# A two-layer mixer and experts kernel: blocks of two sizes, a wide last stage, u·B in two places, gates apart, a table of offsets

## The chip, the cores and the metric

The kernel runs on one core of a Trainium2 chip. The metric is the device time of one execution in microseconds, lower is better. Engines have short names throughout: PE is the matrix engine (PEld its weight loads), DVE the vector engine, ACT the scalar engine, POOL the GpSimd engine, SP the engine that issues most DMAs.

## What is computed

Two layers over x of shape (4, 256, 64, 64), that is 16384 tokens of 256 channels, all in float32. Cut to what matters here:

```python
# layer 0: a Mamba mixer, with d = 512 inner channels and 16 states each
tokens = x_as_tokens @ w_in.T
z = sigmoid(silu(tokens @ w_gate.T + b_gate))
t = layernorm(tokens)
xm, zm = split(t @ in_w.T)
xm = silu(conv4(xm)); dt = softplus(...); B, C = ...
h = exp(dt * A) * h + (dt * xm) * B          # along 4096 tokens, per (channel, state)
y = sum_over_states(h * C) + D * xm
y = (y * silu(zm)) @ out_w.T
x = tokens + (y * z) @ w_out.T + x
# layer 1: a state-space mixer with 8 heads, then a mixture of 8 experts
t = tokens(x);  t = t + mixer1(layernorm(t))
idx = argmax(softmax(layernorm(t) @ gate_w + gate_b)); prb = its probability
pos = place of the token among those of its expert, kept if pos < C = 2560
y_tok = relu(buf @ w1[e] + b1[e]) @ w2[e] + b2[e]   # 256 -> 1024 -> 256
t = t + nan_to_num(y_tok * prb * kept);  out = t as (4, 256, 64, 64)
```

The recurrence of layer 0 is the large part: 4 × 4096 tokens × 512 channels × 16 states.

## The kernel before, in words

Three stages run one after another: the mixers of both layers, the experts, and a last stage that turns token rows into channel rows.

*Mixers.* The tokens go by in 64 chunks of 256 (four images of 16). For each chunk the recurrence is done in 16 units. A unit handles 128 partitions (4 states × 32 channels) and a free size of 4 × 256. In `scan` (from line 837) unit u = j × 4 + f does the following: four ACT exponentials write the decay tile `da`; DVE multiplies `u4` by B (a tensor_tensor) into `ub`, a tile of 4 KB per partition in two banks of PSUM of which there is one copy (`bank_u`, depth 1); if the chunk isn't an image's first, a short DVE tensor_tensor adds the carried state `e0` into the first column of `ub`; DVE runs tensor_tensor_scan over `da` and `ub` into `h` (SBUF, three copies); POOL multiplies `h` by C into `p` (two copies); PE sums `p` over states into `py`. Every second j, `gx`, a tile of gates and of the inputs that pass by the recurrence, is loaded by two DMAs of 256 KB (two copies of 8 KB per partition). ACT writes the passing half, scaled by D, into `py`, and DVE multiplies `py` by the gate half into `g`.

While a chunk's units run, other parts of this chunk and of earlier and later ones are done between them: `front0` and `mid0` (projections, convolution, dt), `tail0`, `front1`, `ssd` and `back1` (layer 1 and the routing). Each part carries a due time in units, set by `k_.at(n)`: the constants `FRONT0`, `MID0`, `TAIL`, `SSD`, `BACK` give the parts their place, and `SHIFT` could give single calls of `at` an offset, by their number within a chunk. It is empty before.

The order of instructions on every engine is planned while the program is built, by the class `Plan`: a list scheduler with a weight for each instruction (`dve`, `act`, `mm`, ...), a delay for a result to be seen by another engine (`SIGNAL`) or by its own (`BEHIND`), the depth of each ring of tiles, and one resource that DVE and POOL share, called the port. A DVE operation holds the port in the plan if more than one of its tensor inputs lies in SBUF; a scan never does. A POOL operation always does. The multiplication by C is marked `ride`: it is put at the start of a scan, and in the program it waits for the DVE instruction just ahead of that scan.

At the end of the mixers, DVE works out from the counts of the experts a table: for each of 71 blocks of 256 rows which rows of the routed buffer it holds (`row_at`) and which expert's weights (`w_at`).

*Experts.* For each block (`begin(i)` and the loop after it, from line 1335): POOL gathers rows and one expert's weights (4360 floats per partition, three buffers) by indirect DMA, ACT normalizes, PE transposes, then PE does the first layer in 8 pieces of 128 hidden channels (ACT and DVE apply bias and relu) and the second layer; DVE and ACT clean up the result, POOL scatters it into `tok_d`. The next block's `begin` is placed in the middle of the first layer.

*Last stage* (`turn`): 32 pieces of 512 tokens. SP loads rows from `tok_d` so that a partition holds every 128th token (runs of 1 KB), PE transposes them, DVE and ACT in turn copy the result out of PSUM, ACT's queue stores 2 KB runs.

Of the kernel before, what the change touches and what calls it, by code (L numbers as in the profile page):

```python
# [20 lines left out]
P = 128  # L21
# [21 lines left out]
MID0 = -16  # L43
TAIL, SSD, BACK = 18, 29, 37
AHEAD = 4

SHIFT = {}
TOK = 4
# [88 lines left out]
class Plan:  # L137
# [6 lines left out]
    SIGNAL = {"DVE": 0.13, "ACT": 0.19, "PE": 0.21, "POOL": 0.12}  # L144
    BEHIND = {"DVE": 0.13, "ACT": 0.14, "PE": 0.0, "POOL": 0.13}
    LANES = 8
# [237 lines left out]
def tile_conv_attn_hybrid(ctx: ExitStack, tc: tile.TileContext, a: dict, out: bass.AP, cap: int, st: int):  # L384
# [12 lines left out]
    def nm(s):  # L397
        return f"{s}_{next(names)}"
# [10 lines left out]
    make_identity(nc, ident)  # L409

    nj = st // P
    nblk = NT // st + NE - 1
    row_at = const.tile([P, nblk, nj], U32, name="row_at")
    w_at = const.tile([P, nblk], U32, name="w_at")

# [10 lines left out]
    def mixers(es):  # L426
# [138 lines left out]
        def work(shape, tag, bufs=1):  # L565
            return r.tile(lambda: wk.tile(shape, F32, name=nm(tag), tag=tag, bufs=bufs), shape, tag, bufs)
# [76 lines left out]

        routed, rows_at, ws_at = r.fixed(buf_d), r.fixed(row_at), r.fixed(w_at)

# [191 lines left out]
        def scan(k_):  # L837
# [10 lines left out]
            for j in range(KD):  # L848
# [11 lines left out]
                if j % 2 == 0:  # L860

                    gx = work([P, 2, 2, T], "gx", 2)
                    for s in range(2):
                        r.dma("SP", gx[:, s], k_.gx_d[s * KD + j : s * KD + j + 2].rearrange("j p l -> p j l"))
                sl = slice(j * SQ, (j + 1) * SQ)
# [7 lines left out]
                for f in range(SQ):  # L873
# [6 lines left out]
                    k_.at(u)  # L880
                    ub = bank_u(SQ, T)
                    r.tt(ub, u4, bc[:, 0, None, :].to_broadcast([P, SQ, T]), ALU.mult)
# [10 lines left out]
                    if f == 0:  # L893
                        if j % 2 == 0:
                            py = bank_y(2, T)
                            for i in range(2):
                                r.act(py[:, i], gx[:, 1, i], AF.Copy, scale=m_d[:, j + i : j + i + 1])
                    for i in range(SQ):
# [11 lines left out]
                if j % 2 == 1:  # L910
                    r.tt(k_.g[:, j - 1 : j + 1], gx[:, 0], py, ALU.mult)

# [374 lines left out]
        def iota(t, step, n, cm=0):  # L1287
            r.gps("iota", t, [[step, n]], 0, cm, allow_small_or_imprecise_dtypes=True)
            return t
# [4 lines left out]

        per = cap // st
        steps, block, which_e = iota(line(0, per), st, per), iota(line(0, nblk), 1, nblk), iota(line(0, NE), 1, NE)
        place = iota(line(0, nj), P, nj, 1)
        counts, one, blocks, ends, starts = (line(0, NE) for _ in range(5))
        which, count, base, limit = (line(0, nblk) for _ in range(4))
        some = line(0, NE, per)  # L1300
        r.gps("memset", one, 1.0)
        r.copy(counts, total)
        r.tt(some, over(counts, (NE, per), True), over(steps, (NE, per), False), ALU.is_gt)
        r.dve("tensor_reduce", blocks, some, AX.X, ALU.add)
        r.dve("tensor_tensor_scan", ends, one, blocks, 0.0, ALU.mult, ALU.add)
        r.tt(starts, ends, blocks, ALU.subtract)
        n = (nblk, NE)
        table = line(1, *n)
        r.tt(table, over(block, n, True), over(ends, n, False), ALU.is_ge)
        r.dve("tensor_reduce", which, table, AX.X, ALU.add)  # L1310
        mine = line(2, *n)
        r.tt(mine, over(which, n, True), over(which_e, n, False), ALU.is_equal)
        for sums, values in ((base, starts), (count, counts)):
            r.tt(table, mine, over(values, n, False), ALU.mult)
            r.dve("tensor_reduce", sums, table, AX.X, ALU.add)

        r.tt(base, block, base, ALU.subtract)
        r.dve("tensor_scalar", base, base, float(st), None, ALU.mult)
        r.dve("scalar_tensor_tensor", count, count, float(cap), base, ALU.min, ALU.subtract)
        r.dve("scalar_tensor_tensor", base, which, float(cap), base, ALU.mult, ALU.add)  # L1320
        r.dve("tensor_scalar", base, base, float(NSLOT), None, ALU.subtract)
        n = (nblk, nj)
        row, valid = line(2, *n), line(2, *n)
        r.tt(valid, over(count, n, True), over(place, n, False), ALU.is_gt)
        r.tt(row, over(base, n, True), over(place, n, False), ALU.add)
        r.tt(row, row, valid, ALU.mult)
        r.dve("tensor_scalar", rows_at, row, float(NSLOT), None, ALU.add)
        r.dve("tensor_scalar", which, which, float(NE - 1), float(P), ALU.min, ALU.mult)
        r.tt(ws_at, which, place[:, :1].to_broadcast([P, nblk]), ALU.add)
        r.issue()  # L1330

    def experts(es):
# [19 lines left out]

        def begin(i):

            w = wp.tile([P, W1 + W2 + KF + C], F32, name=nm("w"), tag="w")
            rows = wk.tile([P, nj, ROW], F32, name=nm("rows"), tag="rows", bufs=4)
            for j in range(nj):
                gather(rows[:, j], buf_d, row_at[:, i, j : j + 1], NSLOT + P)
            gather(w, a["w_exp"], w_at[:, i : i + 1], NE * P)
            tn = wk.tile([P, nj, C], F32, name=nm("tn"), tag="tn")  # L1360
            for j in range(nj):
                act(tn[:, j], rows[:, j, TOK:], AF.Identity, scale=rows[:, j, 1:2], bias=rows[:, j, 2:3])  # L1362
            number = wk.tile([P, nj], U32, name=nm("number"), tag="number", bufs=4)
            nc.vector.tensor_copy(number, rows[:, :, 3])  # L1364
            xt = wk.tile([P, KC, st], F32, name=nm("xt"), tag="xt")
            pt = pt_p.tile([P, KC, st], F32, name=nm("pt"), tag="pt")
            for k in range(KC):
                for j in range(nj):
                    nc.tensor.transpose(pt[:, k, j * P : (j + 1) * P], tn[:, j, k * P : (k + 1) * P], ident)
            nc.vector.tensor_copy(xt, pt)  # L1370
            return w, rows, number, xt

        now = begin(0)
        for i in range(nblk):
            w, rows, number, xt = now
# [3 lines left out]
            b2 = w[:, W1 + W2 + KF :]  # L1379
            hid = wk.tile([P, KF, st], F32, name=nm("hid"), tag="hid")  # L1380
            for f in range(KF):
                if f == KF // 2 and i + 1 < nblk:

                    now = begin(i + 1)
                ph = ph_p.tile([P, st], F32, name=nm("ph"), tag="ph")
                for k in range(KC):
                    mm(ph, w1[:, k, f * P : (f + 1) * P], xt[:, k], start=k == 0, stop=k == KC - 1)  # L1387
                if f % 4 != 3:
                    act(hid[:, f], ph, AF.Relu, bias=b1[:, f : f + 1])  # L1389
                else:  # L1390
                    ts(hid[:, f], ph, b1[:, f : f + 1], 0.0, ALU.add, ALU.max)
            y = wk.tile([P, nj, C], F32, name=nm("y"), tag="y")
            fixed = wk.tile([P, nj, C], F32, name=nm("fixed"), tag="fixed")
            ok = wk.tile([P, nj, C], U32, name=nm("ok"), tag="ok", bufs=1)
            po = po_p.tile([P, nj, C], F32, name=nm("po"), tag="po")
            for j in range(nj):
# [22 lines left out]
    def turn(es):  # L1419

        wk = es.enter_context(tc.tile_pool(name="out_work", bufs=6))
        pt_p = es.enter_context(tc.tile_pool(name="out_ps", bufs=6, space=PSUM))
        W = 512
        nj = W // P
        for b in range(NB):
            for c in range(L // W):
                i = b * L + c * W
                rows = wk.tile([P, nj, C], F32, name=nm("outrows"), tag="outrows")
                nc.sync.dma_start(rows, tok_d[i : i + W].rearrange("(j p) d -> p j d", p=P))  # L1429
                o = wk.tile([P, KC, W], F32, name=nm("o"), tag="o")  # L1430
                for k in range(KC):
                    pt = pt_p.tile([P, W], F32, name=nm("pto"), tag="pto")
                    for j in range(nj):
                        nc.tensor.transpose(pt[:, j * P : (j + 1) * P], rows[:, j, k * P : (k + 1) * P], ident)  # L1434
                    if k % 2 == 0:
                        nc.vector.tensor_copy(o[:, k], pt)  # L1436
                    else:
                        nc.scalar.copy(o[:, k], pt)  # L1438
                nc.scalar.dma_start(out[b].rearrange("(k p) l -> p k l", p=P)[:, :, c * W : (c + 1) * W], o)  # L1439
# [103 lines left out]
```

## Time and profile before

| what | us |
|---|---|
| median of 3 runs | 6741.11 (6736.48 to 6754.15) |
| the profiled execution's own time | 6746.82 |
| its span, first to last instruction | 6745.1 |
| mixers, to the last entry of the routing table | 5611 |
| experts, to the last block's scatter | 5611 to about 6652 |
| last stage | 6653.7 to 6745 |

The span and the shares of the page are of one execution. A group line gives the line of the kernel, the engine, the operation, what it writes and reads, the sizes, the count, the busy time in us with the mean of one in ns, and the idle time of the engine just ahead with what ended most of it. Nearly all the mixers' instructions have line 373, since the planner issues them all from there; so they are told apart by the tiles they write. A window line gives busy time and count for PE, PEld, DVE, ACT and POOL, then the granted clock of PE, the mean busy share of the 16 DMA engines and what they moved in GB/s. Where DVE or POOL is held up inside an instruction, no idle time is shown: the instruction only has a longer duration. The granted clock over the execution was 0.957.

### The profile page before, as it was taken

Reading aid. Unit: us, or ns where it says so; the run is one execution under the profiler, and the core shown is the slowest. Engines: PE = TensorE matmul, PEld = TensorE weight load, DVE = VectorE, ACT = ScalarE, POOL = GpSimd, SP = SyncE. Lnnn points to the kernel's source line nnn. Section 1 sums busy time; section 2 is a strip of 40 time slices with the busy share of each in tenths; the row PEclk is TensorE's granted clock in tenths of the full one; section 3 lists DMA queues with packets and bytes.
Section 4 is the critical chain, followed back from the end, with each engine's and each line's share of the span. In section 5 each row is a group of like instructions: output and inputs, shape, how many; then the busy total and the mean of one; then the engine's idle time right before and its main releaser. Section 6 shows DMA issues by size and latency. Waiting matters only on the chain. (4 is left out here: it accounts for less than half of the span.)

```text
span 6745.1 us, 111880 instructions
## 1 busy us (share of the span) xinstructions
PE 6239.9 (93%) x37672; PEld 4330.6 (64%) x37672; DVE 5559.2 (82%) x7646; ACT 4878.5 (72%) x12007; POOL 3305.5 (49%) x2632
## 2 busy tenths in 40 slices
PE   7899999999999999999999999999999978999996
PEld 5566666666666666666666666666666546888886
DVE  5999999999999999999999999999999973344443
ACT  6888888888878888888888888888888852333332
POOL 4655555555555555555555555555555542333331
PEclk8999999999999999999999999999999988999998
DMA  6855555555555555555555555555555534555556
GB/s 189 233 151 149 151 149 151 149 147 151 152 148 153 149 148 152 152 153 152 149 150 151 151 153 147 156 151 151 153 149 150 148 92 158 186 196 190 193 191 243
DMA packets 943874, 1077.19 MB, mean 160 GB/s; under 512 B 94480, under 2 KB 912404, under 8 KB 934082
## 3 DMA queue, kind: packets, MB, share of 16 engines
q1 hardware_dynamic: 904594, 842.28, 45.0%
q0 software_dynamic: 30000, 210.98, 8.7%
q10 hardware_dynamic: 8704, 16.78, 0.6%
q8 instruction: 297, 4.87, 0.3%
q14 instruction: 279, 2.29, 0.1%
HBM read 785.70 MB, written 277.68 MB: 158 GB/s over the span
## 5 line engine op out<-in xcount | busy, mean ns | idle before, releaser
L373 POOL TENSOR_TENSOR p<-h,bc 128x1024 f32<-128x1024 f32 x1024 | 2413.7, 2357 | 1996.7 <-DVE ub L373 501.3
L373 DVE TENSOR_TENSOR_SCAN h<-da,ub 128x1024 f32<-128x1024 f32 x1024 | 2339.1, 2284 | 77.0 <-ACT da L373 4.4
L373 ACT ACTIVATE da<-dt,w_m_Alog 128x255 f32<-128x255 f32 x4096 | 1842.7, 502 | 0.0
L373 DVE TENSOR_TENSOR ub<-u,bc 128x1024 f32<-128x1024 f32 x1024 | 1279.1, 1249 | 13.9 <-DMA u<-u_d 6.5
L373 PE MATMUL py<-p,sum 128*32 128x256 f32 x8192 | 658.9, 394 | 175.1 <-POOL p L373 168.8
L373 PE MATMUL b<-t,w_W_in 128*128 128x256 f32 x2304 | 579.0, 392 | 25.2 <-ACT bcs L373 4.8
L373 PEld LDWEIGHTS b<-t,w_W_in 128*128 128x128 f32 x2304 | 418.4, 190 | 188.7 <-ACT raw L373 75.3
L1387 PE MATMUL ph<-xt,w 128*128 128x256 f32 x2272 | 516.3, 381 | 4.0 <-ACT hid L1389 3.9
L373 PE MATMUL a<-t,w_m_in_w 128*128 128x256 f32 x2048 | 513.4, 395 | 3.0 <-DVE t L373 2.7
L1398 PE MATMUL po<-w,hid 128*128 128x256 f32 x2272 | 502.0, 379 | 0.0
L373 PEld LDWEIGHTS py<-p,sum 128*32 128x32 f32 x8192 | 169.0, 108 | 497.3 <-POOL p L373 246.5
L373 PE MATMUL a<-raw,taps_m 128*128 128x256 f32 x2048 | 482.0, 383 | 4.9 <-ACT pre L373 4.9
L1398 PEld LDWEIGHTS po<-w,hid 128*128 128x128 f32 x2272 | 431.7, 190 | 58.7
L1387 PEld LDWEIGHTS ph<-xt,w 128*128 128x128 f32 x2272 | 427.0, 191 | 62.2 <-ACT hid L1389 5.7
L373 PEld LDWEIGHTS a<-t,w_m_in_w 128*128 128x128 f32 x2048 | 372.8, 191 | 145.6 <-issue 72.5
L373 PEld LDWEIGHTS a<-raw,taps_m 128*128 128x128 f32 x2048 | 378.2, 190 | 130.4 <-ACT e L373 39.8
L373 ACT COPY hlast<-h 128x4 f32<-128x4 f32 x1024 | 202.9, 198 | 273.6 <-DVE h L373 260.9
L1364 DVE CAST number<-rows 128x2 uint32<-128x2 f32 x71 | 12.0, 169 | 467.0 <-DMA tok_d<-fixed,number 455.5
L1362 ACT ACTIVATE tn<-rows 128x256 f32<-128x256 f32 x142 | 82.3, 597 | 402.9 <-DMA rows<-buf_d,row_at 397.2
L373 PE MATMUL c<-cum,after 128*128 128x512 f32 x512 | 323.8, 719 | 15.9 <-ACT dend L373 13.5
L1410 POOL DMA_INDIRECT tok_d<-fixed,number x142 | 146.1, 1029 | 391.2 <-DVE fixed L1408 308.5
L373 ACT ACT_TABLE_LOAD x256 | 328.4, 1283 | 4.5
(237 smaller groups left out, 11320.5 us busy)
## 6 DMA issues: line engine op xcount, KB each, us to landing
dt<-dt_d SPq DMA_DIRECT2D x1024, 128.0 KB, 2.8
u<-u_d SPq DMA_DIRECT2D x1024, 128.0 KB, 2.2
raw<-raw_d SPq DMA_DIRECT2D x1024, 128.0 KB, 3.6
gx_d<-pre SPq DMA_DIRECT2D x64, 1024.0 KB, 5.5
bc<-bc_d SPq DMA_DIRECT2D x1024, 64.0 KB, 2.4
gx<-gx_d SPq DMA_DIRECT2D x256, 256.0 KB, 4.8
raw_d<-raw SPq DMA_DIRECT2D x64, 518.0 KB, 3.6
dt_d<-mid SPq DMA_DIRECT2D x64, 512.0 KB
```

Of the source, the lines that this page charges most:

```text
L373: op.issued = f(*map(placed, args), **{k: placed(v) for k, v in kw.items()})
L1362: act(tn[:, j], rows[:, j, TOK:], AF.Identity, scale=rows[:, j, 1:2], bias=rows[:, j, 2:3])
L1364: nc.vector.tensor_copy(number, rows[:, :, 3])
L1387: mm(ph, w1[:, k, f * P : (f + 1) * P], xt[:, k], start=k == 0, stop=k == KC - 1)
L1398: mm(po[:, j], hid[:, f, j * P : (j + 1) * P], w2[:, f], start=f == 0, stop=f == KF - 1)
L1410: nc.gpsimd.indirect_dma_start(out=tok_d, out_offset=bass.IndirectOffsetOnAxis(ap=number[:, j : j + 1], axis=0), in_=fixed[:, j], in_offse ...
```

## The change

Five things are changed at once.

1. `ub` of even units is a tile in SBUF (`ub1`, one copy), that of odd units stays in PSUM.
2. `gx` is split in two tiles of 4 KB, `pass` and `gate`, one copy each, with load times of their own. The SBUF that this frees is what `ub1` takes.
3. `SHIFT` gets 13 offsets, `SSD` and `BACK` come one unit earlier, and the plan's delay of a DVE result to DVE (`BEHIND`) goes from 0.13 to 0.17.
4. The experts' 71 blocks of 256 rows become 63 of 256 (two units of 128) and 9 of 128, with a routing table for each size; the small ones are spread among the large.
5. The last stage works on 16 pieces of 1024 tokens. A partition holds 8 consecutive tokens (a run of 8 KB), so the copies out of PSUM write with a stride of 8 elements, and stores go in 4 KB runs.

```diff
-TAIL, SSD, BACK = 18, 29, 37
+TAIL, SSD, BACK = 18, 28, 36
-SHIFT = {}
+SHIFT = {
+    18: -0.2, 41: 0.5, 47: 5.9, 50: -1.7, 51: -0.5, 58: -6.4, 63: 1.1, 97: -0.9, 108: 1.0, 111: 0.2, 120: -9.8,
+    130: -1.0, 137: -0.2,
+}
-    BEHIND = {"DVE": 0.13, "ACT": 0.14, "PE": 0.0, "POOL": 0.13}
+    BEHIND = {"DVE": 0.17, "ACT": 0.14, "PE": 0.0, "POOL": 0.13}
...
     nj = st // P
-    nblk = NT // st + NE - 1
-    row_at = const.tile([P, nblk, nj], U32, name="row_at")
-    w_at = const.tile([P, nblk], U32, name="w_at")
+    units = NT // P + NE - 1
+    n_big = (units - NE) // 2
+    sizes = (nj, n_big), (1, units - nj * n_big)
+    tables = [
+        (const.tile([P, n, k], U32, name=f"row_at{k}"), const.tile([P, n], U32, name=f"w_at{k}")) for k, n in sizes
+    ]
...
-                    gx = work([P, 2, 2, T], "gx", 2)
-                    for s in range(2):
-                        r.dma("SP", gx[:, s], k_.gx_d[s * KD + j : s * KD + j + 2].rearrange("j p l -> p j l"))
+                    both = []
+                    for s, name, n in ((1, "pass", -AHEAD), (0, "gate", 3)):
+                        k_.at(j * SQ + n)
+                        t = work([P, 2, T], name)
+                        r.dma("SP", t, k_.gx_d[s * KD + j : s * KD + j + 2].rearrange("j p l -> p j l"))
+                        both.append(t)
+                    passed, gate = both
...
-                    ub = bank_u(SQ, T)
+                    ub = bank_u(SQ, T) if u % 2 else work([P, SQ, T], "ub1")
...
-                                r.act(py[:, i], gx[:, 1, i], AF.Copy, scale=m_d[:, j + i : j + i + 1])
+                                r.act(py[:, i], passed[:, i], AF.Copy, scale=m_d[:, j + i : j + i + 1])
...
-                    r.tt(k_.g[:, j - 1 : j + 1], gx[:, 0], py, ALU.mult)
+                    r.tt(k_.g[:, j - 1 : j + 1], gate, py, ALU.mult)
...
+        upto_here(ends, starts, pairs)
+        r.dve("tensor_scalar", taken, starts, -1.0, float(n_big), ALU.mult, ALU.add)
+        r.dve("scalar_tensor_tensor", taken, taken, 0.0, pairs, ALU.max, ALU.min)
+        r.dve("scalar_tensor_tensor", rest, taken, -2.0, n_units, ALU.mult, ALU.add)
+        r.dve("tensor_scalar", gone, taken, float(st), None, ALU.mult)
+        for (k, nblk), (rows_at, ws_at), n_blocks, behind in zip(sizes, tables, (taken, rest), (zero_e, gone)):
+            rows_at, ws_at = r.fixed(rows_at), r.fixed(ws_at)
+            upto_here(ends, starts, n_blocks)
...
-        now = begin(0)
-        for i in range(nblk):
+        line_up = sorted(((i + 0.5) / n, k, i) for k, n in sizes for i in range(n))
+        now = begin(*line_up[0][1:])
+        for at, (_, nj, _) in enumerate(line_up):
+            st = nj * P
...
-        wk = es.enter_context(tc.tile_pool(name="out_work", bufs=6))
+        wk = es.enter_context(tc.tile_pool(name="out_work", bufs=4))
-        W = 512
+        W = 1024
         nj = W // P
+        half = nj // 2
...
-                nc.sync.dma_start(rows, tok_d[i : i + W].rearrange("(j p) d -> p j d", p=P))
+                nc.sync.dma_start(rows, tok_d[i : i + W].rearrange("(p j) d -> p j d", p=P))
...
+                    for h in range(2):
+                        pt = pt_p.tile([P, half, P], F32, name=nm("pto"), tag="pto")
+                        for j in range(half):
+                            nc.tensor.transpose(pt[:, j], rows[:, h * half + j, k * P : (k + 1) * P], ident)
+                        to = o[:, k].rearrange("c (p j) -> c j p", j=nj)[:, h * half : (h + 1) * half]
```

The rest of the routing table (which expert a block belongs to, its rows) is worked out as before, once for each of the two sizes.

## The prediction

> **What bounds the kernel now.** I read the page first, then the chain of waits, the windows, the groups by form, and last the timeline.
>
> ```profile
> span 6745.1 us, 111880 instructions
> PE 6239.9 (93%) x37672; PEld 4330.6 (64%) x37672; DVE 5559.2 (82%) x7646; ACT 4878.5 (72%) x12007; POOL 3305.5 (49%) x2632
> ```
>
> The shares mix three stages. The chain of waits doesn't help: its 73 pieces begin at 6624 us, inside the last stages. So I go by windows (busy time and count of PE, PEld, DVE, ACT, POOL; clock; DMA share; GB/s):
>
> ```profile
> 4760.00:4930.00 170.00, 159.46 (x1017) 103.98 (x1016) 160.96 (x216) 141.31 (x353) 93.07 (x71) 0.97 0.55 155
> ...
> 5655.00:6650.00 995.00, 984.25 (x4685) 864.22 (x4683) 408.82 (x762) 316.76 (x686) 347.12 (x338) 1.00 0.52 185
> ...
> 6695.00:6715.00 20.00, 12.66 (x72) 10.82 (x71) 5.57 (x9) 3.85 (x8) 0.00 (x0) 0.76 1.08 385
> ```
>
> The mixers (to 5611 us) keep DVE at 161 of 170 us and PE at 159, the experts (to 6650) keep PE at 99%, and the last stage keeps the DMA engines full at 385 GB/s. The mixers hold four fifths of the span. Their costliest groups:
>
> ```profile
> L373 POOL TENSOR_TENSOR p<-h,bc 128x1024 f32<-128x1024 f32 x1024 | 2413.7, 2357 | 1996.7 <-DVE ub L373 501.3
> L373 DVE TENSOR_TENSOR_SCAN h<-da,ub 128x1024 f32<-128x1024 f32 x1024 | 2339.1, 2284 | 77.0 <-ACT da L373 4.4
> ...
> L373 DVE TENSOR_TENSOR ub<-u,bc 128x1024 f32<-128x1024 f32 x1024 | 1279.1, 1249 | 13.9 <-DMA u<-u_d 6.5
> ```
>
> The tile view of h has the first scan at 82.4 us and the last at 5506.2: 5424 us for 1024 units, 5.30 us a unit, 84.8 us for a chunk of 16. POOL's p takes 2.36 us per unit, and whether it fits beside DVE decides everything below. The timeline shows when it does and when it doesn't (start, duration, engine):
>
> ```profile
> 394.50 2.36 POOL L373 TENSOR_TENSOR p<-h,bc 128x1024 f32<-128x1024 f32 x1 [0.69 <-DVE cdec L373]
> ...
> 395.54 2.40 DVE L373 TENSOR_TENSOR decay<-decay,gm 128x1024 f32<-128x1024 f32 x1
> 396.80 1.19 POOL L373 COPY raw<-tail_raw 128x12 f32<-128x12 f32 x1
> ...
> 397.86 0.67 DVE L373 TENSOR_TENSOR g<-gx,py 128x512 f32<-128x512 f32 x1
> 398.11 2.36 POOL L373 TENSOR_TENSOR p<-h,bc 128x1024 f32<-128x1024 f32 x1
> 398.46 3.10 DVE L373 TENSOR_TENSOR ub<-u,bc 128x1024 f32<-128x1024 f32 x1
> ...
> 5475.84 2.29 DVE L373 TENSOR_TENSOR_SCAN h<-da,ub 128x1024 f32<-128x1024 f32 x1
> 5476.07 2.35 POOL L373 TENSOR_TENSOR p<-h,bc 128x1024 f32<-128x1024 f32 x1 [2.11 <-DVE de L373]
> ```
>
> decay and ub have both inputs in SBUF. Started while p runs they take 2.40 and 3.10 us, and end 1.1 us after p does: they stood still. A copy of 12 elements on POOL, caught behind decay, takes 1.19 us (0.2 elsewhere). The scan, whose ub lies in PSUM, runs beside p at full speed for both.
>
> **What the Trainium skill says.** "SBUF — State Buffer", section "Who interferes with whom": a DVE instruction with two SBUF inputs contends with a GpSimd instruction that reads SBUF, since its second input comes through the read interface they share; whoever comes first holds it for the whole instruction. The lines above agree for tensor_tensor. "VectorE: DVE Perf Modes", section "Two Vector instructions with no wait between them", names tensor_tensor_scan beside tensor_tensor among the operations with two SBUF inputs. No scan of the kernel before with two long inputs in SBUF shows whether it locks too; that is the open point.
>
> **The change, part by part.**
>
> *u·B in two places.* Every even unit writes ub to SBUF ("ub1"), every odd one to PSUM. Removed: the wait of the next ub for the scan that still reads the one bank. Added: 512 scans with da and ub both in SBUF. The planner still treats a scan as free of the port and starts p just behind the scan's start: in the timeline above p comes 0.23 us after its scan. With the lock the p of each odd unit, which rides an even scan, is shut out, and enters at the first DVE instruction that doesn't need the lock; behind it, the next one that does waits. I walked one chunk of the changed order on DVE and POOL by hand (the order in which the changed program issues), with these durations: ub 1.13 from start to start, scans 2.2, p 2.36, small ones 0.1 to 0.2. A typical stretch: even scan 0 to 2.2; its p enters at the fix-up of the odd unit (one SBUF input) and runs 2.2 to 4.56; the next short instruction with two SBUF inputs waits till 4.56; ub to 5.8; the odd scan covers the following p. Where the fix-up is followed directly by the odd scan, that scan covers the late p, but the next p then starts as it ends and stops the next ub for 2.3 us. So of two p's one is covered and one not. Over the eight pairs of a chunk the stops are 2.2, 0.4, 2.35, 2.35, 2.3, 0.4, 1.7, 0.9, 2.1, 0.1 and 2.1: 16.9 us. Of these some 1.5 us exist already (decay has mean 1870 ns against 1219 undisturbed, two a chunk). The second ub and longer gaps take back part of DVE's present 4.5 idle us a chunk (170 − 161, halved): I take 2. Net +13.4 us × 64 = **+858 us**. Bounds: perfect packing leaves lock time alone, per chunk on DVE 16 × 1.23 (ub) + 8 × 2.28 (even scans) + some 14 (mid, decay, cdec, xdt, state and short ones), on POOL 16 × 2.36 + 3, sum 92.8 against 84.8: +510. All eight late p's in full and nothing taken back: 18.9, +1210. If a scan doesn't lock, the part gains instead: half of those 4.5 to 5 idle us, 2.6 × 64 = −166 (0 to −290).
>
> *Gates apart, offsets, constants.* gx in two single buffers, the same two DMAs of 256 KB for each second j, now 4 units ahead and 3 behind; g waits for its gate with ub and scans queued behind it on DVE. The median of a gx landing is 4.8 us, and five units lie between issue and use: nothing. The offsets and ssd/back one unit earlier only reorder DVE, ACT, PE and SP, and their effect is inside the estimate above; the last chunk's tail (5506 to 5611 us) may lose 5 us by it: 0 taken.
>
> *Routing table.* Two tables instead of one: some 22 more short dependent DVE instructions on the path between last scan and first gather, 0.2 to 0.3 us each (rows there start 0.21 apart): +6.
>
> *Blocks of two sizes.* 71 blocks of 256 become 63 of 256 and 9 of 128. PE sets this stage:
>
> ```profile
> 6017.36 3.62 PE L1387 MATMUL ph<-xt,w 128*128 128x256 f32 x16
> ...
> 6020.82 7.07 PE L1398 MATMUL po<-w,hid 128*128 128x256 f32 x32
> ...
> 6663.78 1.06 PE L1434 MATMUL pto<-ident,outrows 128*128 128x128 f32 x8 [0.25 <-DMA outrows<-tok_d]
> ```
>
> A big block takes 14.26 us (po to po, 6006.56 to 6020.82). A small one: 32 ph at the 0.133 us that 128 columns take in the last line, 16 po at 0.221, two transposes: 8.1. So 63 × 14.26 + 9 × 8.1 = 971 against 1012: −41. But a weight gather (4360 × 128 × 4 bytes = 2.23 MB) and the 5.6 us from row gather to tn now face an 8 us block: PE may wait up to 4 us behind each of nine, −5 at worst. I take −25.
>
> *Wide last stage.* 91 us for 2 × 16.8 MB at about 388 GB/s. Reads become 8 KB runs, writes 4 KB. The skill, "DMA: Bandwidth & Descriptors", section "Where 436 GB/s comes from", sets 435 as ceiling: at best 86.5 → 77 us, −9. Against it the first 1 MB must land before anything turns and the last leaves as 1 MB: some +3 each by the 6.5 us that 512 KB takes. Copies with a stride of 8 elements have cover (DVE 5.6 of 20 us). Taken: −3 (−9 to +8).
>
> Sum: 858 + 6 − 25 − 3 = +836. The profiled execution took 6746.82 us for its span of 6745.1, 0.1% above the median of 6741.11; onto the median this gives 7577, in round figures **7575 us**.
>
> **Rivals.** (a) *The scan doesn't lock*, faster: it takes 2.2 ns an element where the tensor_tensor of ub takes 1.2, which might leave the interface free half the time, and the planner exempts it by name. Against: short scalar_tensor_tensor instructions with two SBUF inputs (hot, red) also take 0.29 to 0.40 instead of 0.16 us beside p, so the lock isn't a matter of tensor_tensor alone. Time: 6741 − 166 + 6 − 25 − 3 = 6553 (6450 to 6700). It decides from the first even scan. (b) *No lock, and PE at 159 of 170 us is the next bound*: nothing gained in the mixers, 6719. (c) *The lock, but mostly covered*: late p's fall into idle time, a third of the cost: 6741 + 290 − 22 = 7009.
>
> **How the numbers follow.** Lock in full 0.69 (7575, own range 7250 to 7850), (a) 0.22, (b) 0.05, (c) 0.04. A measurement of this kernel tells some 0.3% from no change. Slower: 0.69 + 0.04 = 0.73; faster: 0.22 and 0.03 of (b); the same: 0.02. To leave no more than 2 in 10 out, the range must reach down into half of (a): 6560 to 7800.
>
> **What would show it.** Right: p's mean still near 2.36 us but DVE instructions with two SBUF inputs (ub, decay, ex) at means well above 1.25, or p itself stretched to 4 us when it comes behind an even scan; windows of 170 us with 28 scans instead of 32; DVE waiting for POOL before scans. Wrong: p beginning 0.25 us after an even scan and both at 2.3 us, with ub at 1.23. The experts are right if PE's window there ends some 25 us sooner, the last stage if its GB/s rises above 390.

## The result, and the profile after

The changed kernel takes 7269.73 us (median of 4 runs, 7262.32 to 7279.37), the kernel before 6742.75 in the runs beside it: a ratio of 1.078 (95% interval 1.0761 to 1.08), 527 us slower. The first lines of its page:

```profile
span 7260.3 us, 111754 instructions
PE 6312.3 (87%) x37578; PEld 4421.1 (61%) x37578; DVE 6198.4 (85%) x7685; ACT 4928.9 (68%) x11999; POOL 4312.4 (59%) x2622
```

DVE is busy 639 us longer with 39 more instructions, POOL 1007 us longer with 10 fewer. Nothing like that much work was added, so instructions last longer. The windows view says in which stage (columns as before: busy time and count of PE, PEld, DVE, ACT, POOL, then clock, DMA share, GB/s):

```profile
4760.00:4930.00 170.00, 150.61 (x891) 100.97 (x883) 155.31 (x194) 119.64 (x306) 103.69 (x62) 0.90 0.47 138
6200.00:7160.00 960.00, 947.62 (x4627) 833.91 (x4626) 389.62 (x774) 304.99 (x683) 337.92 (x329) 1.00 0.54 196
7195.00:7215.00 20.00, 11.58 (x50) 9.34 (x48) 6.54 (x7) 6.73 (x7) 0.00 (x0) 0.59 1.02 426
```

In the mixers DVE is busy for 155 of 170 us, about as before (161), but ends 194 instructions instead of 216, and POOL needs 104 us for 62 where 71 took 93. The experts still keep PE at 99%, and the last stage now moves 426 GB/s instead of 385. The three costliest groups of POOL and DVE in the mixers:

```profile
L376 POOL TENSOR_TENSOR p<-h,bc 128x1024 f32<-128x1024 f32 x1024 | 3015.5, 2948 | 1699.5 <-DVE ub L376 313.8
L376 DVE TENSOR_TENSOR_SCAN h<-da,ub 128x1024 f32<-128x1024 f32 x1024 | 2519.4, 2463 | 83.3 <-issue 36.4
L376 DVE TENSOR_TENSOR ub<-u,bc 128x1024 f32<-128x1024 f32 x1024 | 1488.2, 1463 | 7.5 <-DMA u<-u_d 6.5
```

Three small groups of DVE in the same stage, first in the kernel before, then in the changed one:

```profile
L373 DVE SCALAR_TENSOR_TENSOR row<-mv,row 128x2 f32<-128x2 f32 x62 | 10.4, 168 | 3.4 <-ACT row L373 0.7
L373 DVE TENSOR_TENSOR ex<-hot,base_slot 128x16 f32<-128x16 f32 x62 | 18.0, 290 | 0.1
L373 DVE TENSOR_TENSOR dest<-red,n_slots 128x2 uint32<-128x2 f32 x62 | 9.7, 157 | 0.0
```

```profile
L376 DVE SCALAR_TENSOR_TENSOR row<-mv,row 128x2 f32<-128x2 f32 x62 | 125.4, 2022 | 1.5 <-ACT row L376 1.5
L376 DVE TENSOR_TENSOR ex<-hot,base_slot 128x16 f32<-128x16 f32 x62 | 106.7, 1721 | 0.0
L376 DVE TENSOR_TENSOR dest<-red,n_slots 128x2 uint32<-128x2 f32 x62 | 100.7, 1625 | 0.0
```

p went from a mean of 2357 to 2948 ns, the scan from 2284 to 2463, ub from 1249 to 1463. The three small ones have 2 to 16 elements a partition and went from means of 168, 290 and 157 ns to 2022, 1721 and 1625. The idle time ahead of them is nearly nothing, which is how a lock (one engine shuts the other out of something they share until its instruction is through) looks in such a view: the engine has begun and stands still. The timeline shows how both sides lose (start, duration, engine; in brackets what the engine had waited for):

```profile
3186.91 2.37 POOL L376 TENSOR_TENSOR p<-h,bc 128x1024 f32<-128x1024 f32 x1
3187.00 4.42 DVE L376 TENSOR_TENSOR_SCAN h<-da,ub 128x1024 f32<-128x1024 f32 x1
...
3195.53 2.36 POOL L376 TENSOR_TENSOR p<-h,bc 128x1024 f32<-128x1024 f32 x1 [6.25 <-DVE ub L376]
3195.68 2.27 DVE L376 TENSOR_TENSOR_SCAN h<-da,ub 128x1024 f32<-128x1024 f32 x1
...
3200.25 2.28 DVE L376 TENSOR_TENSOR_SCAN h<-da,ub 128x1024 f32<-128x1024 f32 x1
3200.50 4.18 POOL L376 TENSOR_TENSOR p<-h,bc 128x1024 f32<-128x1024 f32 x1 [2.62 <-PE py L376]
3202.45 2.24 DVE L376 SCALAR_TENSOR_TENSOR row<-mv,row 128x2 f32<-128x2 f32 x1
3204.61 0.16 DVE L376 TENSOR_TENSOR ex<-row 128x16 f32<-128x16 f32 x1
```

The first and third scans are of even units (ub in SBUF), the second is of an odd one. In the first pair p came 0.09 us ahead: it ends on time at 3189.28, and the scan lasts 2.14 us beyond that, nearly its own undisturbed length. In the second pair both run undisturbed. In the third the scan came first: p ends 2.15 us after the scan does, and the instruction on 2 elements behind the scan stands still until p is through.

Over all units the records divide as follows. 338 p's began in an even scan, 330 of them were stretched (mean of the 338: 4129 ns); 413 began in an odd scan, mean 2363; 273 beside no scan, mean 2370. Of the 512 even scans 106 took over 2.4 us, mean 4061; none of the odd ones did. In all 106 p had begun first, and that p kept its length; the 8 unstretched p's in even scans began in the last 0.06 us of the scan.

The granted clock of PE fell as well (0.957 to 0.928 over the execution). It doesn't explain the loss: DVE stands idle for less of the stretch between first and last scan than before, 276 us instead of 361, so it isn't kept waiting by a slower PE. By stage, in the two profiled executions:

| stage | before, us | after, us | difference |
|---|---|---|---|
| first scan to last scan | 5423.8 | 5982.4 | +558.6 |
| last scan to end of routing table | 105.3 | 107.9 | +2.6 |
| experts, first ph to last po | 1019.3 | 982.9 | −36.4 |
| last stage, first pto to end | 87.4 | 79.7 | −7.7 |
| rest (start, gaps between stages) | 109.3 | 107.4 | −1.9 |

The sum is +515, the difference of the two spans (7260.3 − 6745.1).

### The profile page after: what moved, and what is told of

Same layout as the page of the kernel before. It is cut to its first block, busy times and chain, and to the rows that moved or that the text cites. A ratio compares the mean times of both kernels' runs of the same rounds, so it can differ in the third digit from the quotient of the medians.

```text
span 7260.3 us, 111754 instructions
## 1 busy us (share of the span) xinstructions
PE 6312.3 (87%) x37578; PEld 4421.1 (61%) x37578; DVE 6198.4 (85%) x7685; ACT 4928.9 (68%) x11999; POOL 4312.4 (59%) x2622
## 3 DMA queue, kind: packets, MB, share of 16 engines
q14 instruction: 279, 2.29, 0.1%
## 5 line engine op out<-in xcount | busy, mean ns | idle before, releaser
L376 POOL TENSOR_TENSOR p<-h,bc 128x1024 f32<-128x1024 f32 x1024 | 3015.5, 2948 | 1699.5 <-DVE ub L376 313.8
L376 DVE TENSOR_TENSOR_SCAN h<-da,ub 128x1024 f32<-128x1024 f32 x1024 | 2519.4, 2463 | 83.3 <-issue 36.4
L376 DVE TENSOR_TENSOR ub<-u,bc 128x1024 f32<-128x1024 f32 x1024 | 1488.2, 1463 | 7.5 <-DMA u<-u_d 6.5
L376 PE MATMUL py<-p,sum 128*32 128x256 f32 x8192 | 684.0, 414 | 423.4 <-POOL p L376 417.7
L376 PE MATMUL b<-t,w_W_in 128*128 128x256 f32 x2304 | 669.5, 438 | 77.0 <-ACT bcs L376 33.8
L376 PEld LDWEIGHTS b<-t,w_W_in 128*128 128x128 f32 x2304 | 475.6, 216 | 269.7 <-ACT raw L376 77.5
L376 PE MATMUL a<-raw,taps_m 128*128 128x256 f32 x2048 | 517.5, 402 | 6.8 <-ACT pre L376 6.8
L1418 PE MATMUL ph<-xt,w 128*128 128x256 f32 (+1 forms) x2304 | 496.6, 368 | 12.4 <-ACT hid L1420 12.0
L1429 PE MATMUL po<-w,hid 128*128 128x256 f32 x2160 | 478.3, 379 | 0.0
L1429 PEld LDWEIGHTS po<-w,hid 128*128 128x128 f32 x2160 | 410.1, 190 | 55.4
```

The lines of the kernel that those rows point to most:

```text
L376: op.issued = f(*map(placed, args), **{k: placed(v) for k, v in kw.items()})
L1429: mm(po[:, j], hid[:, f, j * P : (j + 1) * P], w2[:, f], start=f == 0, stop=f == KF - 1)
```

## Experiments

The theory: an even scan, with da and ub both in SBUF, and POOL's p, which reads h and C from SBUF, exclude each other, and this alone costs the 559 us. Rivals: the orders changed with it (offsets, due times, split gates) cost the time; ub in SBUF is slow in itself, or its writing is in the way; the plan is merely bad because it doesn't know of the lock. "Stops" below are the durations of DVE instructions beyond those of the same group when undisturbed, summed from first to last scan: 108 us in the kernel before, 883 in the changed one. These sums shift by up to some 30 us with what is taken as undisturbed. Runs given by one time were made once, with a profile.

**1. Everything but ub in SBUF.**

```diff
-                    ub = bank_u(SQ, T) if u % 2 else work([P, SQ, T], "ub1")
+                    ub = bank_u(SQ, T)
```

> The changed kernel with ub of every unit in the one PSUM tile again; gates apart, offsets, constants, two block sizes and the wide last stage stay. Theory (the scan with both inputs in SBUF shuts POOL's p out): the scans' stretch goes from 5982 us back to about that of before (5424, within 60), no scan is longer than 2.4 us, no p longer than 2.5 us, and with the 36 us of the experts and 8 us of the last stage the time is 6700, between 6640 and 6760. Rival (the offsets and the new order cost the time, not the place of ub): it stays above 7000.

Measured: 6714.47 us (median of 5, ratio to before 0.9965, interval 0.9951 to 0.9979), stretch of the scans 5432 us, stops 119. Its groups:

```profile
L376 POOL TENSOR_TENSOR p<-h,bc 128x1024 f32<-128x1024 f32 x1024 | 2412.5, 2356 | 1651.2 <-DVE mid L376 407.6
L376 DVE TENSOR_TENSOR_SCAN h<-da,ub 128x1024 f32<-128x1024 f32 x1024 | 2339.6, 2285 | 85.6 <-ACT da L376 29.0
L376 DVE TENSOR_TENSOR ub<-u,bc 128x1024 f32<-128x1024 f32 x1024 | 1319.7, 1289 | 14.1 <-DMA u<-u_d 6.5
```

p and scan are back at 2356 and 2285 ns: one line of the change carries the loss, and with all else kept the kernel is a little faster than before.

**2. The reverse: only ub1, and the split gates that make room for it, in the kernel before.**

```diff
-                    ub = bank_u(SQ, T)
+                    ub = bank_u(SQ, T) if u % 2 else work([P, SQ, T], "ub1")
```

> The kernel before with nothing but ub of even units in SBUF and the gates apart (which makes its room); no offsets, old constants, one block size, old last stage. Theory: the scans' stretch is about 5980 us again (5900 to 6150), about a hundred even scans last 4 us, time about 7300. Rival (the order made by offsets and constants is at fault): about 6750 or, through the second ub, below.

Measured: 7355.16 us, stretch 6032, stops 890. The tile views of h and p (count: shortest, median, longest in ns, first and last start):

```profile
L373 DVE TENSOR_TENSOR_SCAN h<-da,ub x1024: 2254/2279/4472, 82.7 to 6114.6; 128x1024 f32<-128x1024 f32 x171
L373 POOL TENSOR_TENSOR p<-h,bc x1024: 2339/3412/4423, 87.3 to 6123.1; 128x1024 f32<-128x1024 f32 x171
```

The loss is there without the offsets, the earlier `ssd` and `back` and the longer delay. The split gates are here too, but experiment 1 has them without a loss. (By the shapes in the diff of the change, a copy of `gx` takes 4 KB per partition and `pass` and `gate` 2 KB each; the description ahead of the prediction gives twice that. The 4 KB set free are what `ub1` takes.) Who bears the loss differs from what was expected: 498 p's began in even scans and were all stretched, which lifts the median of p to 3412, while only 13 even scans were long, not about a hundred. In the changed kernel the order lets p come first more often. So the number of long scans isn't a mark of the lock by itself; p's and scans have to be counted together. The offsets and due times take back 50 us of stretch here (6032 to 5982), in one profiled execution each.

**3. The p's of odd units, which the plan puts at the start of even scans, on DVE.**

```diff
-                    r.gps("tensor_tensor", p, h, bc[:, 1, None, :].to_broadcast([P, SQ, T]), ALU.mult, ride=True)
+                    if u % 2:
+                        r.tt(p, h, bc[:, 1, None, :].to_broadcast([P, SQ, T]), ALU.mult)
+                    else:
+                        r.gps("tensor_tensor", p, h, bc[:, 1, None, :].to_broadcast([P, SQ, T]), ALU.mult, ride=True)
```

> The changed kernel with p of odd units, those that ride a scan with both inputs in SBUF, computed by DVE instead of POOL. Theory: the stops of DVE in the mixers (883 us) nearly vanish and eight multiplications of 1.15 us a chunk (589 us) come in their place: scans' stretch about 5982 - 774 + 589 = 5800 us, time about 7080. Rival (the second ub or the order costs the time, and p is a bystander): DVE only gets more work, 7260 + 400 or more.

Measured: 7027.39 us, stretch 5757, stops 54. The two kinds of p:

```profile
L376 POOL TENSOR_TENSOR p<-h,bc 128x1024 f32<-128x1024 f32 x512 | 1211.1, 2365 | 1270.9 <-DVE stats L376 349.0
...
L376 DVE TENSOR_TENSOR p<-h,bc 128x1024 f32<-128x1024 f32 x512 | 630.3, 1231 | 0.4 <-PE py L376 0.2
```

ub1 is still written and scanned, yet most of the stops are gone and the even scans have a mean of 2.29 us, and DVE is quicker with 630 us of extra work than with the lock. So an even scan, its ub or the writing of ub in SBUF isn't slow in itself; it has to meet a p.

**4. p only written.**

```diff
-                    r.gps("tensor_tensor", p, h, bc[:, 1, None, :].to_broadcast([P, SQ, T]), ALU.mult, ride=True)
+                    r.gps("memset", p, 0.0, ride=True)
```

> The changed kernel with p filled with zeros by POOL instead of h times C: left out is the multiplication by C, so the recurrence adds nothing to y. POOL's instruction writes SBUF and reads none of it. Theory (the lock is on the read side): even scans and the fills overlap, no scan is longer than 2.4 us, DVE's stops fall from 883 us to under 100, and the time is at or below 6700. Rival (any POOL instruction on SBUF excludes a DVE instruction with two SBUF inputs): stops remain in proportion to the fills' duration.

Measured: 6933.44 us; stops below 0.01 us, no scan above 2.4 us. An even scan with POOL's writing beside it, and a POOL copy beside a DVE tensor_tensor just before, in the timeline:

```profile
3001.03 1.22 DVE L376 TENSOR_TENSOR mid<-mid,mid 128x1024 f32<-128x1024 f32 x1
3001.19 1.10 POOL L376 COPY tail_rbc<-rbc 128x3 f32<-128x3 f32 x1 [5.41 <-ACT rbc L376]
3002.16 2.28 DVE L376 TENSOR_TENSOR_SCAN h<-da,ub 128x1024 f32<-128x1024 f32 x1
3002.39 0.95 POOL L376 MEMSET p<- 128x1024 f32 x1
```

The scan is of an even unit. The copy of 3 elements, which reads SBUF, is held until mid is through; the MEMSET, which writes 1024, isn't. The exclusion is on reading, as "SBUF — State Buffer" of the Trainium skill, section "Who interferes with whom", states. The time is a miss, 230 us above the bound expected. In the view of waits POOL's queue now stands still for other reasons:

```profile
POOL p L376 <- PE py L376: 790.1, 269, 10.8
POOL e L376 <- ACT e L376: 588.9, 160, 9.2
POOL tail_raw L376 <- ACT raw L376: 464.3, 125, 37.2
```

DVE is idle for 821 us of the stretch instead of 276. The plan was made anew for a POOL with other work. That this new order causes the idle time is argued from the waits; no run isolates it. The run settles the mechanism, not the price.

**5. The plan is told of the lock.** A scan with two inputs in SBUF takes the port in the plan, so p isn't put beside it.

```diff
-            n, port = 2 * n, False
+            n = 2 * n
```

> The changed kernel, with one thing told to its planner: a scan whose two inputs both lie in SBUF holds the port for its duration, so no p is placed beside an even scan. If the lock itself is the cost, this moves the 512 p's away from the even scans but finds little free room for them: the bound from lock time alone is 92.8 us a chunk (84.8 before, 93.5 in the changed kernel), so the scans' stretch stays at 5850 to 6000 us and the time at 7130 to 7290, with the stops of DVE down from 883 to under 250 us and POOL or DVE idle in their place. If the cost was only that the plan didn't know of the lock, the stretch falls near that of the kernel before, 5430 to 5550, and the time to about 6720 to 6830.

Measured: 7375.57 us, stretch 6089, stops 709; slower than either theory said, and the stops aren't under 250. Its p group and POOL's longest wait:

```profile
L376 POOL TENSOR_TENSOR p<-h,bc 128x1024 f32<-128x1024 f32 x1024 | 2532.5, 2476 | 2618.8 <-DVE ub L376 1063.8
```

```profile
POOL p L376 <- DVE ub L376: 1063.8, 256, 9.1
```

Only 3 p's now begin in an even scan, and p's own mean falls to 2476. But 691 begin beside no scan, where DVE's other instructions with two SBUF inputs meet them: 121 even scans are long (mean 3717 ns), since p was already running when they began, three small groups stop for about 100 us each, and DVE is idle 512 us besides. Told in this way, the plan doesn't buy the time back, so "the plan doesn't know" isn't the cause by itself; a plan whose times fit the run more closely wasn't tried. My bound of 5850 to 6000 was too low, since it counted lock time alone and no idle time.

**6. A dose: every fourth unit's ub in SBUF.**

```diff
-                    ub = bank_u(SQ, T) if u % 2 else work([P, SQ, T], "ub1")
+                    ub = bank_u(SQ, T) if u % 4 else work([P, SQ, T], "ub1")
```

> The changed kernel with u B in SBUF for every fourth unit instead of every second: 256 scans with two inputs in SBUF instead of 512. If the loss is so many late p's at a price for each, half of it is left: stretch 5432 + 275 = 5707 (5620 to 5790), time about 6990 (6900 to 7070), stops of DVE between 400 and 560 us. If wider gaps between the locked scans let idle time take up the late p's, the loss is well under half and the time below 6850.

Measured: 6993.45 us, stops 421, and from the tile view of h a stretch of 5713.5 us:

```profile
L376 DVE TENSOR_TENSOR_SCAN h<-da,ub x1024: 2247/2286/4469, 81.1 to 5794.6; 128x1024 f32<-128x1024 f32 x171
```

Half the locked scans, half the loss (281 of 550 us over experiment 1). Counting p's stretched in an even scan and even scans made long together, 229 cases here cost 281 us of stretch, 436 in the changed kernel 550, 511 in experiment 2 608 (against the kernel before): 1.23, 1.26 and 1.19 us each. In these three orders, then, a p that meets a locked scan goes with a loss of about half of its own 2.36 us. It is an average that takes in the stops of other instructions and DVE's idle time, not a fixed price: experiment 5 has only 124 such cases and loses 657 us over experiment 1.

**7. The two late stages alone, and the orders without ub1.** First, the kernel before with blocks of two sizes and the wide last stage only:

```diff
+    n_big = (units - NE) // 2
+    sizes = (nj, n_big), (1, units - nj * n_big)
...
-        W = 512
+        W = 1024
```

> The kernel before with only the blocks of two sizes and the wide last stage; the mixers as before. By what these stages took in the changed kernel (experts 1019.3 to 982.9, last stage 87.4 to 79.7, table 105.3 to 107.9): 6742 - 36 - 8 + 3 = 6700, 6690 to 6712; by the terms of the prediction it would be 6742 - 25 - 3 + 6 = 6720.

Second, experiment 1 without the offsets and due times (gates stay split):

```diff
-TAIL, SSD, BACK = 18, 28, 36
+TAIL, SSD, BACK = 18, 29, 37
...
-    BEHIND = {"DVE": 0.17, "ACT": 0.14, "PE": 0.0, "POOL": 0.13}
+    BEHIND = {"DVE": 0.13, "ACT": 0.14, "PE": 0.0, "POOL": 0.13}
...
-                    ub = bank_u(SQ, T) if u % 2 else work([P, SQ, T], "ub1")
+                    ub = bank_u(SQ, T)
```

The 13 offsets of SHIFT are taken out in the same run.

> The changed kernel with u B in PSUM for all units and without the table of offsets, the unit by which ssd and back come earlier and the longer delay; gates apart stay. If these orderings are worth nothing without ub1, as the prediction took, it agrees with the run that only had u B put back (6714) within 0.3 percent, and its scans' stretch is 5432 +- 20 us; if the offsets help by themselves it is slower than that one by 15 us or more; if they harm without ub1, for which they may be made, it is faster, down to 6695.

Measured: the late stages alone 6702.95 us (median of 5, ratio 0.9933, 0.9919 to 0.9946), as the sum of the measured stages had it and not the prediction's 6720; without offsets 6694.18 (median of 5, ratio 0.9928, 0.9914 to 0.9942), stretch 5412. The windows of the first run, in its last stage and its experts:

```profile
6640.00:6660.00 20.00, 11.93 (x56) 10.11 (x56) 7.21 (x8) 7.54 (x8) 0.00 (x0) 0.67 1.02 424
5640.00:6600.00 960.00, 948.32 (x4621) 833.42 (x4620) 387.91 (x771) 305.46 (x682) 338.44 (x329) 1.00 0.54 196
```

From first ph to last po it takes 983.9 us and its last stage 79.8, as in the changed kernel (982.9 and 79.7): what these two stages take doesn't depend on the change to the mixers. Splitting the gates adds nothing that can be told apart (6694 and 6703, intervals overlap). The offsets, the new due times and the longer delay cost time without ub1: the ratio without them, 0.9928, lies clear of the 0.9965 with them (each against the kernel before in the runs beside it), some 20 to 25 us. The third of the three expectations holds: together with ub1 they took back 50 us (one profiled execution each), without it they are better left out. Which of the three does it wasn't tried. The kernel without them is the fastest of the study beside the one with the late stages alone; both are faster than the kernel before by 0.7%.

What a second ub is worth where nothing is shut out stays open: the two runs with it and few stops or none, experiments 3 and 4, have other work on DVE or a new order with much idle time.

## Why the prediction held, point by point

*The open point.* The prediction rested on whether tensor_tensor_scan with two long inputs in SBUF locks out POOL's reads, for which it had only the Trainium skill's general sentence. The timeline after and experiments 1, 3 and 4 show that it does, for the whole instruction and in both directions. (That section says of another kind of DVE instruction, its 2-port modes, that the first to issue holds the lock for its whole length; that it is so for two SBUF inputs is shown here by the 330 stretched p's and 106 stretched scans.) Rivals (a) and (b), without a lock, are out. Of (c), mostly covered, a part came true: 559 of the 858 us came, about midway between the estimate and (c)'s 290.

The stated range, 6560 to 7800, reached over nearly every outcome that was considered, so a time inside it says little. The measured 7270 is just inside the lower end of the range given for the lock itself (7250 to 7850). What held is the mechanism and the sign.

*The sum of the mixers: right in sign and kind, 300 us too large.* The accounts of DVE between first and last scan: its durations sum to 5459.9 us before and 6199.6 after, +739.7. Of this the records overlap by 96.5 more (in them an instruction with no wait begins some 0.08 us before the end of the one ahead), and idle time falls by 84.6 (360.6 to 276.0). That leaves +558.6. In the terms of the prediction, per chunk:

| term | predicted, us | measured, us |
|---|---|---|
| growth of durations (16.9 of stops, less 1.5 that existed) | 15.4 | 11.6 |
| taken back by DVE's gaps (measured: 1.3 of idle time, 1.5 of overlap between records) | 2.0 | 2.8 |
| net | 13.4 | 8.7 |

The term that was mis-sized is the first, and in it the number of cases more than the price of each. I let all eight p's of odd units in a chunk ride an even scan and be late: 512. The run has 330 stretched p's and 106 stretched scans, 436, or 6.8 a chunk; the other p's began in an odd scan or beside none. All stops together, 883 us, are 2.0 for each case, close to the 2.1 of the walk (16.9 over 8); both still hold what existed before. My lower bound, pure lock time without any loss of packing, was +510, and the kernel came out only 49 above it. One step of the walk was wrong in detail: p doesn't wait for an instruction that leaves the port free. It gets in as soon as the scan ends, even where the next DVE instruction wants the port (the row instruction in the timeline). A slip in rival (a) changes nothing here: half of 4.5 to 5 idle us is 2.25 to 2.5, not 2.6.

*Gates, offsets, constants: 0 predicted.* Right for the gates. The offsets aren't nothing, but −50 with ub1 and +20 to +25 without; the tail of the last chunk, for which up to 5 us was thought possible, belongs to the +2.6 below.

*Routing table: +6 predicted.* Last scan to table's end: +2.6 in the changed kernel. With the late stages alone (experiment 7), which has the second table and the old mixers, it is 105.1 us against 105.3 before: the table's extra instructions cost nothing that one execution shows, so the +2.6 seems to come with the mixers' part.

*Blocks of two sizes: −25 predicted, −36.4 measured.* The count of PE work (−41) was close: PE's busy time from first ph to last po fell from 1015.3 to 970.5 us, by 45. The mis-sized term is the allowance of 16 us for slow gathers: PE's waits grew by 8 us, and not for gathers. In the view of PE's waits within the experts the one thing that grew is ph waiting for ACT's hid, from 3.9 to 12.0 us.

*Wide last stage: −3 predicted, −7.7 measured.* In the middle of the stage the rate rose from 385 to 426 GB/s, near the 435 that the prediction took as ceiling from the Trainium skill, "DMA: Bandwidth & Descriptors", section "Where 436 GB/s comes from". The same section puts transfers between HBM (the memory outside the core) and SBUF under a limit of about 358 GB/s; on this one core both rates lie above it, and the measurement decides. Runs and pieces grew together, so which of them raised the rate isn't shown. The longer first load lies ahead of the first pto: the gap from the last po grew from 14.5 to 15.6 us, so that the stage with its first load gained 6.5. The +3 at either end were the mis-sized terms; the first cost about 1 us, the last wasn't separated.

Of the signs named in advance, p stretched to 4 us behind an even scan, small instructions at many times their length, and a last stage above 390 GB/s are there; 170 us hold 29 scans (5982.4 us for 1023) where 28 were foreseen. DVE waiting for POOL ahead of scans hardly shows (26 us in all), since the stop lies inside the instruction.

## What to carry to other kernels

Before moving an operand from PSUM to SBUF, count which instruction then has two SBUF inputs on DVE, and what POOL reads at that time: an operand in PSUM may be what lets two engines run side by side. Look for this lock in durations, not in idle time, and first in the smallest instructions of DVE, where 2 elements taking 2.2 us stand out at once. A large change should be read by stages: here two parts worth −44 us together were buried under one worth +550, and the new order that won 50 us back beside it cost 20 to 25 without it.

## What was unexpected of the hardware

- The lock changes hands at the end of an instruction in favour of the engine that waits. No p of the changed kernel took longer than 4.43 us, its own 2.36 and the better part of one scan, even where DVE had another instruction with two SBUF inputs next, as in the timeline.
- A lead of less than 0.1 us decides who pays: p ahead of the scan by 0.09 cost the scan 2.14 us, the scan ahead by 0.25 cost p 1.8 and the instruction behind the scan 2.1. The shortest leads in the records of the changed kernel are 0.07 us for p and 0.02 for the scan, and there too the later one was stretched.
- A locked pair didn't cost its full length in three of the runs: DVE's stretch grew by 1.2 us for each of them, about half of p's 2.36, at counts of 229, 436 and 511. Experiment 5, where p's met DVE's other instructions instead, doesn't follow this.
